# A feature-crossing kernel: SyncE's fill of the first table waits for the second chunk's weights, and the second block's x is loaded behind the last second-half gather

## The chip, the cores and the metric

The kernel runs on one core of a Trainium2 chip. The metric is the device time of one execution in microseconds; the profile adds the span of one profiled execution, counted from the program's first instruction to its last. A core has five engines that run side by side and wait for each other through semaphores: TensorE (PE in the profile; PEld is its weight load), VectorE (DVE), ScalarE (ACT), GpSimd (POOL) and SyncE (SP). Transfers between the device's memory and the on-chip memory are issued by SP, ACT or POOL and carried by the core's 16 DMA engines.

## What is computed

Three layers of a compressed interaction network over x of 1024 samples, 39 fields and 64 embedding columns, then a linear layer over the sums:

```
def _cin_layer(Xk, X0, W, b):
    O = W.shape[0]
    Hk, Fdim = (Xk.shape[1], X0.shape[1])
    Wr = W.reshape(O, Hk, Fdim)
    return jnp.einsum('bhe,bfe,ohf->boe', Xk, X0, Wr) + b[None, :, None]
...
Xk = X0
outs = []
for W, b in ((W0, b0), (W1, b1), (W2, b2)):
    Xk = _cin_layer(Xk, X0, W, b)
    outs.append(Xk.sum(axis=-1))
cin_output = jnp.concatenate(outs, axis=-1)
return cin_output @ fc_w.T + fc_b
```

Everything is float32, and the result has one number for each sample.

## The kernel before

The first layer needs every product of two fields. The kernel folds the weights of all three layers into weights for those pairs at the start, and then works on blocks of 32 samples (2048 columns, a column being one embedding position of one sample). For each block it gathers rows of x into tables of 128 partitions, so that the product of two tables holds 128 pairs of fields at once. Five tables r[0] to r[4] per block, and two small ones u and v per two blocks, cover all pairs. There are 32 blocks, handled in twos: 16 pairs.

**Chunks.** A chunk is one product of two tables (`product`, line 213, on DVE), followed by four matmuls of 128x512 with that chunk's weights (`multiply`, line 555, on TensorE). A block has six chunks; chunk c multiplies tables (0,1), (0,2), (3,1), (3,2), (0,4) and (3,4) in this order, so tables 0 to 3 serve the first four chunks and table 4 is first used by the fifth. The first block of each pair has a seventh step, the product of u and v, for both blocks together (`join`, line 567). The products run four steps ahead of the matmuls (`AHEAD`, line 652) and use four buffers. When a block is done, `finish` (line 613) takes the sums out of the accumulators with ScalarE and VectorE; in the program's order, it stands before the product of the next block's fifth chunk.

**Where the rows come from.** Row gathers read from a table `xd` in device memory, with x laid out by field (40 rows a block: 39 fields and a row of ones; 80 rows for two blocks). There are three such tables, used in turn. A direct load (`load`, line 166) writes one block of x into a table as 1248 runs of 64 numbers. For the very first block there is a shorter way: `load_half` brings its two halves (16 samples, 1024 columns each) into the small tables `xh[0]` and `xh[1]`, and tiles 0 to 3 are gathered from these, half by half (loop at line 389, eight gathers). The first big table is then filled in three ways: the row of ones by `fill_ones(0, ...)`, the first block by copies of the two halves (line 396), and the second block by `load(1)`. Out of it come tile 4 of the first block (`roll(0, (4,))`), u and v (`roll_small(0)`) and the five tiles of the second block (`roll(1)`).

**Order.** The program is scheduled by hand: every engine executes its instructions in the order in which the function records them. POOL issues the indirect gathers (line 174) and some direct DMAs, SP and ACT the others. An instruction that waits holds up what stands behind it on the same engine. Before the change, POOL's order at the start is: `fill_ones(0)`; the four gathers of the first half; two of the second half; `load(1)`; the other two of the second half; tile 4; u; v; the five tiles of the second block; four small loads of biases (b0s, b1s, b2s, fcb); the ones of table 2. SP's order is: the row fc_w; the copies of half 1 and half 0 into table 0, which wait for the halves only; the ones of table 1, which wait for a copy of the ones that ACT makes (line 709); and the loads of blocks 2, 3 and so on.

**TensorE's order at the start.** The weights' preparation; a transpose of chunk 0's weights (`weight_turn`, line 536, whose result two ACT copies at lines 544 and 545 carry over); the first quarter of chunk 0; the transpose of chunk 1's weights; the second quarter of chunk 0 and the first of chunk 1; the transpose for chunk 2; and so on to the main loop at line 689.

```
    for k, (n, c) in enumerate(steps[:3]):
        multiply(n, c, p[n, c], (0,))
        if k < 2:
            weight_turn(steps[k + 1][1])
        multiply(n, c, p[n, c], (1,))
```

Of the kernel before, what the change touches and what calls it, by code (L numbers as in the profile page):

```python
# [54 lines left out]
F32 = mybir.dt.float32  # L55
# [5 lines left out]
B, F, E, H = 1024, 39, 64, 64  # L61
# [25 lines left out]
NY = 3  # L87
# [60 lines left out]
def cin_kernel(ctx: ExitStack, tc: tile.TileContext, x, w0t, b0, w1, b1, w2, b2, fc_w, fc_b, out):  # L148
    nc = tc.nc
# [3 lines left out]
    const = ctx.enter_context(tc.tile_pool(name="const", bufs=1))  # L153
# [6 lines left out]
    xd = [dram.tile([2 * FT, BLK], F32, name=f"xd{k}") for k in range(NTAB)]  # L160
    xh = [dram.tile([F, SUB], F32, name=f"xh{k}") for k in range(2)]

    def bank(name):
        return psum.tile([128, MM], F32, name=name, tag="po")

    def load(n, engine=nc.sync):
        first = n % 2 * FT
        engine.dma_start(  # L168
            xd[n // 2 % NTAB][first : first + F].rearrange("f (b e) -> f b e", e=E),
            xv[:, n * BB : (n + 1) * BB, :],  # L170
        )

    def gather_rows(dst, table, k):
        nc.gpsimd.indirect_dma_start(  # L174
            dst, None, table, bass.IndirectOffsetOnAxis(ap=lists[:, k : k + 1], axis=0)
        )

    def roll(n, tiles=range(NT)):
        for i in tiles:
            k = n % 2 * NT + i  # L180
            gather_rows(rt[n % 2][:, i], xd[n // 2 % NTAB][: FT if k < NT else 2 * FT], k)

    def roll_small(n):
        table = xd[n // 2 % NTAB].rearrange("f (t c) -> (f t) c", c=SUB)
        for k, dst in enumerate((ut, vt)):
            gather_rows(dst[n // 2 % 2], table, 2 * NT + k)
# [6 lines left out]
    b2s = const.tile([H, 1], F32, name="b2s")  # L193
    b1s = const.tile([128, 1], F32, name="b1s")
    b0s = const.tile([128, 1], F32, name="b0s")
    fc0s = columns[:, 1:2]
    fcb = const.tile([NY * 32, 1], F32, name="fcb")
# [7 lines left out]

    ones = const.tile([16, 2, 128], F32, name="ones")
    ones1 = const.tile([16, 2, 128], F32, name="ones1")

    both = const.tile([128, F * FT], F32, name="both")
    pairs = const.tile([128, NCHUNK, 128], F32, name="pairs")  # L210
# [2 lines left out]
    def product(n, c, cols=slice(0, BLK), p=None):  # L213
        if p is None:
            p = prods.tile([128, BLK], F32, name="p", tag="p")
        if c < NPAIR:
            i, k = PAIRS[c]
            r = rt[n % 2]
            nc.vector.tensor_tensor(p[:, cols], r[:, i, cols], r[:, k, cols], ALU.mult)  # L219
        else:  # L220
            nc.vector.tensor_tensor(p[:, 0:SUB], ut[n // 2 % 2], vt[n // 2 % 2], ALU.mult)  # L221
        return p

    prep = tc.tile_pool(name="prep", bufs=1)
    with prep as prep:
# [142 lines left out]
        def fill_ones(k, engine, src):  # L368
            engine.dma_start(xd[k][F::FT].rearrange("r (p c) -> p r c", c=128), src)

        fill_ones(0, nc.gpsimd, ones)


        nc.vector.tensor_scalar(unit, apart, 0, None, ALU.is_equal)
        for h in (0, H):
# [13 lines left out]
        halves = [slice(0, SUB), slice(SUB, BLK)]  # L389
        for k, cols in enumerate(halves):  # L390
            for i in range(4):
                gather_rows(rt[0][:, i, cols], xh[k], i)
                if k and i == 1:
                    load(1, nc.gpsimd)
        for k in (1, 0):
            nc.sync.dma_start(xd[0][0:F, halves[k]], xh[k])
        roll(0, (4,))

# [70 lines left out]
        nc.vector.tensor_tensor(both_of[:, 0:1], most, jumps[:, 0:1], ALU.add)  # L471
        nc.vector.tensor_tensor(both_of[:, 1:2], both_of[:, 0:1], jumps[:, 1:2], ALU.add)
        nc.vector.tensor_scalar(lists[:, 2 * NT :], both_of, 2.0, seat, ALU.mult, ALU.add)
        roll_small(0)
        roll(1)
        for h in (0, H):
            nc.gpsimd.dma_start(b0s[h : h + H], b0.rearrange("(h o) -> h o", o=1))
        nc.gpsimd.dma_start(b1s, b1.rearrange("(h o) -> h o", o=1).to_broadcast([H, 2]))
        nc.gpsimd.dma_start(b2s, b2.rearrange("(h o) -> h o", o=1))
        nc.gpsimd.dma_start(  # L480
            fcb, fc_b.rearrange("(p o) -> p o", o=1).to_broadcast([NY * 32, 1])
        )
        fill_ones(2, nc.gpsimd, ones)
        w1v = w1s.rearrange("o (h f) -> o h f", f=F)
        groups = [(k, min(NA * k, F - NA)) for k in range(4)]
        for k, a in groups:
# [49 lines left out]
    def weight_turn(c):  # L536
        place = len(turned) % 4 * 128
        if not place:
            tr = bank("tr")
        else:  # L540
            tr = turned[-1]
        turned.append(tr)
        nc.tensor.transpose(tr[:, place : place + 128], pairs[:, c], unit)  # L543
        nc.scalar.copy(wa[:, c, 0 : 2 * H], tr[:, place : place + 2 * H])  # L544
        nc.scalar.copy(wa[:, c, 2 * H :], tr[:, place : place + H])
# [5 lines left out]
    def open_block(n):  # L551
        if n not in po:
            po[n] = [bank("po") for _ in range(BLK // MM)]

    def multiply(n, c, p, quarters=range(BLK // MM)):
        open_block(n)
        for m in quarters:
            side = m % 2 * H
            nc.tensor.matmul(  # L559
                po[n][m],  # L560
                wa[:, c, side : side + 2 * H],
                p[:, bass.ts(m, MM)],
                start=n % 2 == 0 and c == 0,
                stop=n % 2 == 1 and c == NPAIR - 1,
            )
# [94 lines left out]
    p = {}  # L660
# [19 lines left out]
    weight_rows(c)  # L680
    p[n, c] = product(n, c, halves[0])
    product(n, c, halves[1], p[n, c])
    for k, (n, c) in enumerate(steps[:3]):
        multiply(n, c, p[n, c], (0,))
        if k < 2:
            weight_turn(steps[k + 1][1])
        multiply(n, c, p[n, c], (1,))

    for at, (n, c) in enumerate(steps[:-TAIL]):
# [116 lines left out]
```

## Time and profile before

| | us |
|---|---|
| median of 3 runs | 733.25 |
| the runs | 733.25, 735.53, 732.84 |
| the profiled execution | 733.14 |
| its span | 731.4 |
| TensorE busy in the span | 724.7 |
| VectorE busy | 638.3 |
| GpSimd busy | 397.6 |
| ScalarE busy | 166.9 |

The profiled execution's own time is 1.7 us above its span, which leaves out what lies before the first and after the last instruction. The granted TensorE clock was 0.997 of full speed over the span.

A row of the timeline has the start, the time from the start of the first instruction merged into it to the end of the last, the engine, the line, the operation, its tiles, how many instructions were merged, and in brackets the idle time of the engine ahead of it with what ended it. A DMA row is its issue, not its transfer. Transfers are seen in the DMA view: the queue q0 is GpSimd's, q1 is SyncE's and q10 is ScalarE's, and for GpSimd's issues the view also has the time from the issue to the landing.

### The profile page before, as it was taken

The page shows a single profiled execution, that of the slowest core. Times are in us where ns is not written, and L with a number is a line of the kernel's source. Part 1 is how long each engine was busy: PE and PEld are TensorE (multiplying, and loading weights), DVE is VectorE, ACT ScalarE, POOL GpSimd, SP SyncE. Part 2 cuts the span into 40 slices and gives each one's busy share as a digit, 9 for nine tenths or more (in the row PEclk, how much of TensorE's full clock was granted, in tenths as well). Part 3 has the DMA queues.
Part 4 walks back from the last instruction along what each step waited for, and adds up shares of the span by engine and source line. Part 5 has one row for each costly group of instructions (what it writes and reads, how often), then busy time and mean ns, then how long its engine had stood idle before and what let it go on. Part 6 is the DMA issues. An engine that isn't in the chain of part 4 may idle for free.

```text
span 731.4 us, 6351 instructions
## 1 busy us (share of the span) xinstructions
PE 724.7 (99%) x2375; PEld 316.1 (43%) x2375; DVE 638.3 (87%) x521; ACT 166.9 (23%) x240; POOL 397.6 (54%) x254
## 2 busy tenths in 40 slices
PE   8999999999999999999999999999999999999998
PEld 4444444444444444444444444444444444444443
DVE  6999798988889988889988889888898988889885
ACT  3332121222212222221222212222121221212222
POOL 6789886536555445754537555455654547545300
PEclk9999999999999999999999999999999999999999
DMA  8997899789575887757679675896767777565700
GB/s 268 376 337 280 315 342 356 290 307 338 232 273 231 281 336 286 270 225 285 269 288 330 223 289 219 304 348 236 268 256 274 301 287 266 224 252 236 288 0 0
DMA packets 65983, 197.24 MB, mean 270 GB/s; under 512 B 40110, under 2 KB 40179, under 8 KB 45984
## 3 DMA queue, kind: packets, MB, share of 16 engines
q0 software_dynamic: 28784, 185.56, 65.5%
q1 hardware_dynamic: 35468, 9.29, 5.5%
q10 hardware_dynamic: 1700, 1.99, 1.0%
q8 instruction: 18, 0.29, 0.1%
q14 instruction: 13, 0.11, 0.0%
HBM read 196.76 MB, written 10.60 MB: 284 GB/s over the span
## 4 chain that ended last, share of the span: by engine, by line
PE 99%; DVE 0%; DMA 0%; issue 0%; ACT 0%; DVEq 0%
PE po L559 91%; PE po L579 4%; PE po L590 2%; PE idle L279 0%; PE pv L406 0%; PE pt L487 0%; PE small L323 0%; PE pv L487 0%; PE pw L418 0%; DMA fcrow<-in_fc_w 0%; PE tr L543 0%; DVE g L609 0%; DVE pairs L526 0%; DVE sums L631 0%; ACT z L607 0%
## 5 line engine op out<-in xcount | busy, mean ns | idle before, releaser
L559 PE MATMUL po<-p,wa 128*128 128x512 f32 x1536 | 666.0, 594 | 0.0
L219 DVE TENSOR_TENSOR p<-r 128x2048 f32<-128x2048 f32 (+2 forms) x198 | 434.1, 2224 | 72.4 <-PE po L559 67.1
L559 PEld LDWEIGHTS po<-p,wa 128*128 128x128 f32 x1536 | 290.5, 190 | 371.7 <-issue 354.6
L174 POOL DMA_INDIRECT r<-xd,lists x156 | 302.3, 1938 | 267.1 <-issue 266.2
L607 ACT ACTIVATE z<-po,columns 64x512 f32<-64x512 f32 x128 | 87.3, 682 | 380.1 <-PE po L590 217.9
L609 DVE SCALAR_TENSOR_TENSOR g<-po,b0s,z 64x512 f32<-64x512 f32 x128 | 95.9, 749 | 9.3 <-ACT z L607 5.3
L602 ACT COPY g<-r 39x1024 f32<-39x1024 f32 x64 | 66.7, 1043 | 155.0 <-DVE sums L620 126.8
L620 DVE TENSOR_REDUCE sums<-g 103x16 f32<-103x1024 f32 x62 | 75.6, 1220 | 2.1
L174 POOL DMA_INDIRECT u<-xd,lists x16 | 38.9, 2432 | 7.5 <-issue 4.6
L174 POOL DMA_INDIRECT v<-xd,lists x16 | 38.5, 2403 | 4.9 <-issue 4.9
L579 PE MATMUL po<-p,wa 32*64 32x512 f32 x512 | 31.6, 600 | 0.0
L221 DVE TENSOR_TENSOR p<-u,v 128x1024 f32<-128x1024 f32 x16 | 19.5, 1218 | 0.0
L579 PEld LDWEIGHTS po<-p,wa 32*64 32x64 f32 x512 | 9.4, 131 | 20.2 <-issue 19.4
L590 PE MATMUL po<-u,wa 32*64 32x512 f32 x256 | 17.0, 587 | 0.0
L174 POOL DMA_INDIRECT r<-xh,lists x8 | 8.0, 996 | 4.8 <-DVE tmp L387 2.7
L590 PEld LDWEIGHTS po<-u,wa 32*64 32x64 f32 x256 | 5.7, 132 | 8.0 <-issue 8.0
L526 DVE TENSOR_TENSOR pairs<-both 128x2 f32<-128x2 f32 (+27 forms) x59 | 6.1, 171 | 0.2
L544 ACT COPY wa<-tr 128x128 f32<-128x128 f32 x8 | 2.1, 266 | 16.2 <-PE tr L543 16.2
L279 PE MATMUL idle<-const-float32-1.0 128*128 128x256 f32 (+1 forms) x8 | 4.0, 596 | 0.8 <-PEq L793 0.8
L543 PE MATMUL tr<-unit,pairs 128*128 128x128 f32 x8 | 2.4, 294 | 2.2 <-DVE pairs L526 2.2
L543 PEld LDWEIGHTS tr<-unit,pairs 128*128 128x128 f32 x8 | 1.2, 151 | 4.7 <-ACT pairs L524 2.7
L168 POOL DMA_DIRECT2D xd<-in_x x3 | 3.2, 1055 | 0.0
(97 smaller groups left out, 56.7 us busy)
## 6 DMA issues: line engine op xcount, KB each, us to landing
xd<-in_x SPq DMA_DIRECT2D x28, 312.0 KB
r<-xd,lists POOLq DMA_INDIRECT x156, 8.9
xd<-in_x POOLq DMA_DIRECT2D x3, 312.0 KB, 7.6
w2s<-in_w ACTq DMA_DIRECT2D x1, 624.0 KB
w1s<-in_w ACTq DMA_DIRECT2D x1, 624.0 KB
w0s<-in_w0t ACTq DMA_DIRECT2D x1, 380.2 KB
xh<-in_x ACTq DMA_DIRECT2D x2, 156.0 KB
xd<-xh SPq DMA_DIRECT2D x2, 156.0 KB
```

The source lines that it names most:

```text
L174: nc.gpsimd.indirect_dma_start(dst, None, table, bass.IndirectOffsetOnAxis(ap=lists[:, k : k + 1], axis=0))
L219: nc.vector.tensor_tensor(p[:, cols], r[:, i, cols], r[:, k, cols], ALU.mult)
L221: nc.vector.tensor_tensor(p[:, 0:SUB], ut[n // 2 % 2], vt[n // 2 % 2], ALU.mult)
L279: nc.tensor.matmul(idle[:, 0:cols], nc.const_aps.tensor(1.0, (128, 128), F32), nc.const_aps.tensor(1.0, (128, cols), F32), start=True, sto ...
L526: nc.vector.tensor_tensor(out, diagonal(a, b, sa, sb), diagonal(b, a, sb, sa), ALU.add)
L559: nc.tensor.matmul(po[n][m], wa[:, c, side : side + 2 * H], p[:, bass.ts(m, MM)], start=n % 2 == 0 and c == 0, stop=n % 2 == 1 and c == NP ...
L579: nc.tensor.matmul(dst[half * H : half * H + H], wa[rows, NPAIR, at : at + H], p[rows, bass.ts(side, MM)], start=t >= 2, stop=t < 2 and ha ...
L590: nc.tensor.matmul(dst[half : half + H], wa[rows, NPAIR + 1, H : 2 * H], ut[n // 2 % 2][rows, bass.ts(side, MM)], start=False, stop=t < 2,)
L602: nc.scalar.copy(gt[H : H + F], rt[n % 2][0:F, 0, bass.ts(m, SUB)])
L607: nc.scalar.activation(z[one], po[n][m][other], AF.Identity, bias=fc0s[other])
L609: return lambda: nc.vector.scalar_tensor_tensor(g[n][m // 2][0:H, at], po[n][m][one], b0s[one], z[one], ALU.add, ALU.mult)
L620: nc.vector.tensor_reduce(sums[:, b_at : b_at + SB], g[n][m // 2].rearrange("p (b e) -> p b e", e=E), AX.X, ALU.add,)
```

## The change

SyncE's fill of the first table is put into a function, `fill_table`, which is called right after the transpose of the second chunk's weights. In it a copy of the ones is made on ScalarE (`ones0`), and SyncE's DMA of that copy is now the first of its three DMAs into table 0; so they wait for ScalarE to reach that point of its order, behind the copies of the second chunk's weights. Before, the ones went out on GpSimd, from `ones` itself, and SyncE's copies waited for the halves alone. The instructions of GpSimd that follow (tile 4, u and v, the second block's tiles, the biases, the ones of table 2) stand in the same order as before and are recorded in `fill_table`, too. `load(1)` moves from between the second and third gathers of the second half to behind the fourth.

```diff
@@ const tiles
     ones1 = const.tile([16, 2, 128], F32, name="ones1")
+    ones0 = const.tile([16, 2, 128], F32, name="ones0")
@@ preparation
-        fill_ones(0, nc.gpsimd, ones)
...
         for k, cols in enumerate(halves):
             for i in range(4):
                 gather_rows(rt[0][:, i, cols], xh[k], i)
-                if k and i == 1:
-                    load(1, nc.gpsimd)
-        for k in (1, 0):
-            nc.sync.dma_start(xd[0][0:F, halves[k]], xh[k])
-        roll(0, (4,))
+        load(1, nc.gpsimd)
...
-        roll_small(0)
-        roll(1)
-        for h in (0, H):
-            nc.gpsimd.dma_start(b0s[h : h + H], b0.rearrange("(h o) -> h o", o=1))
...
-        fill_ones(2, nc.gpsimd, ones)
@@ after the products of the first four chunks
+    def fill_table():
+        nc.scalar.copy(ones0, ones)
+        fill_ones(0, nc.sync, ones0)
+        for k in (1, 0):
+            nc.sync.dma_start(xd[0][0:F, halves[k]], xh[k])
+        roll(0, (4,))
+        roll_small(0)
+        roll(1)
+        for h in (0, H):
+            nc.gpsimd.dma_start(b0s[h : h + H], b0.rearrange("(h o) -> h o", o=1))
...
+        fill_ones(2, nc.gpsimd, ones)
+
     for k, (n, c) in enumerate(steps[:3]):
         multiply(n, c, p[n, c], (0,))
         if k < 2:
             weight_turn(steps[k + 1][1])
+        if k == 0:
+            fill_table()
         multiply(n, c, p[n, c], (1,))
```

More of the change, by code (lines that the diff above doesn't have):

```diff
@@ L473, in cin_kernel @@
         nc.vector.tensor_scalar(lists[:, 2 * NT :], both_of, 2.0, seat, ALU.mult, ALU.add)
-        roll_small(0)
-        roll(1)
-        for h in (0, H):
-            nc.gpsimd.dma_start(b0s[h : h + H], b0.rearrange("(h o) -> h o", o=1))
[L478 to L482, printed above, removed]
-        fill_ones(2, nc.gpsimd, ones)
         w1v = w1s.rearrange("o (h f) -> o h f", f=F)
@@ L682, in cin_kernel @@
     product(n, c, halves[1], p[n, c])
+    def fill_table():
[8 more added lines that the diff above has]
+            nc.gpsimd.dma_start(b0s[h : h + H], b0.rearrange("(h o) -> h o", o=1))
+        nc.gpsimd.dma_start(b1s, b1.rearrange("(h o) -> h o", o=1).to_broadcast([H, 2]))
+        nc.gpsimd.dma_start(b2s, b2.rearrange("(h o) -> h o", o=1))
+        nc.gpsimd.dma_start(
+            fcb, fc_b.rearrange("(p o) -> p o", o=1).to_broadcast([NY * 32, 1])
+        )
+        fill_ones(2, nc.gpsimd, ones)
     for k, (n, c) in enumerate(steps[:3]):
```

## The prediction

> **What bounds the kernel now.** I read the page's busy line first, then the chain of waits in order of time, then the first 60 us engine by engine on the timeline, and last the DMA view in short windows. All durations below are of the one profiled execution (733.14 us, span 731.4); the median of the runs is 733.25, so a change worked out on the span can be added to the median as it stands.
>
> ```profile
> PE 724.7 (99%) x2375; PEld 316.1 (43%) x2375; DVE 638.3 (87%) x521; ACT 166.9 (23%) x240; POOL 397.6 (54%) x254
> ```
>
> TensorE is busy all the time. A busy TensorE can hide waits inside modelled matmuls, so the chain has to confirm it (start, length, what; all us):
>
> ```profile
> 15.39 0.37 DVE pairs L526 x3
> ...
> 16.30 0.14 issue
> 16.43 0.30 PE tr L543
> 16.73 0.61 PE idle L279 x2
> 17.34 1.82 PE po L559 x2
> 19.16 0.21 PE tr L543
> 19.38 2.23 PE po L559 x4
> ...
> 21.71 6.87 PE po L559 x16
> ...
> 43.06 41.40 PE po L559 x96
> ```
>
> From 16.43 to 726.24 every piece is TensorE's, with no wait between. 41.40 us for 48 matmuls of 128x512 (two passes each, 96) is 0.8625 us a matmul; the sixteen passes at 21.71 keep the same pace (6.87/16 = 0.43). Only the first six run slower, 1.82 for two passes and 2.23 for four: 1.5 us more than at the later pace. The windows view gives a granted clock of 0.50 from 18 to 20 us, so that is the clock and not a wait for data. Before 16.43 the chain holds the weights' preparation on PE, DVE and ACT, and of DMAs the small row fcrow only. So the x traffic that the change moves is not on the path now. It can come onto it, and to see how far away it is one needs POOL's and DVE's order:
>
> ```profile
> 17.10 1.25 POOL L174 DMA_INDIRECT r<-xh,lists  x1 [0.31 <-issue]
> 18.65 1.66 POOL L174 DMA_INDIRECT r<-xd,lists  x1 [0.30 <-issue]
> 23.23 0.94 POOL L174 DMA_INDIRECT u<-xd,lists  x1 [2.92 <-DVE p L219]
> 24.47 0.95 POOL L174 DMA_INDIRECT v<-xd,lists  x1 [0.30 <-issue]
> 25.73 0.96 POOL L174 DMA_INDIRECT r<-xd,lists  x1 [0.30 <-issue]
> ```
>
> ```profile
> 23.38 2.50 DVE L219 TENSOR_TENSOR p<-r 128x1024 f32<-128x1024 f32 x2 [0.72 <-DMA r<-xh,lists]
> ...
> 29.77 2.28 DVE L219 TENSOR_TENSOR p<-r 128x2048 f32<-128x2048 f32 x1
> ...
> 37.22 2.29 DVE L219 TENSOR_TENSOR p<-r 128x2048 f32<-128x2048 f32 x1 [0.39 <-DMA r<-xd,lists]
> 39.80 2.29 DVE L219 TENSOR_TENSOR p<-r 128x2048 f32<-128x2048 f32 x1 [0.29 <-DMA r<-xd,lists]
> 42.42 4.50 DVE L219 TENSOR_TENSOR p<-r 128x2048 f32<-128x2048 f32 x2 [0.33 <-DMA r<-xd,lists]
> ...
> 52.35 11.09 DVE L219 TENSOR_TENSOR p<-r 128x2048 f32<-128x2048 f32 x5
> ```
>
> POOL idles 2.92 us before u. The label says DVE, but the instruction also waits for the landing of block 1's load, issued at 14.45 with 7.6 us to landing, and the program text has that dependence. DVE waits 0.72 us for a second-half gather, then three times for the gathers of the other set of tables (block 1's): those are DMA-paced, one every 2.6 us.
>
> [...]while SyncE's two copies moved (14 to 17.2 us) their queue took 25.7% of the engines and POOL's fell to 75.6%, from 93.6% in 10.2 to 14.[...]
>
> **The change, part by part.**
>
> 1. fill_ones(0) leaves POOL (0.76 us at 3.70). POOL then waits 2.71 us, until 7.17, for lists and half 0. Gain nothing.
>
> 2. load(1) goes behind the last second-half gather: it costs POOL 1.06 us plus 0.3, so the third and fourth gathers (15.81, 17.10) are issued some 1.06 us earlier. SyncE's 312 KB also leave the DMA engines in 14 to 17.2 us: 25.7% of 3.2 us is 0.8 us of all engines. Load(1)'s own place in the queue was 1.1 us (landings: 13.51 + 7.5 = 21.0, 14.45 + 7.6 = 22.1). So the third gather lands about 1.9 us earlier than 23.3 and DVE's 0.72 us wait is gone. TensorE needs that product (chunk 1, third quarter) at 21.71 + 5 x 0.8625 = 26.0, and half of the 2.50 us pair is done by 24.6: slack 1.4. Gain on the path nothing; what is late next is DVE's product of chunk 4.
>
> 3. The copy into ones0 on ACT: 0.40 us, by the same copy at line 709. ACT is free from 19.79 and idle until 21.75, 1.96 us. Cost nothing; without this cover it would delay the third chunk's weights by 0.4.
>
> ```profile
> 19.57 0.22 ACT L545 COPY wa<-tr 128x64 f32<-128x64 f32 x1
> 21.75 0.27 ACT L544 COPY wa<-tr 128x128 f32<-128x128 f32 x1 [1.96 <-PE tr L543]
> ```
>
> 4. SyncE now waits for that copy, to 20.2. It issues the ones (0.35) and the two copies (1.70, as at 10.13), and is done at 22.3. Queued behind are the ones of table 1 and the loads of blocks 2 and 3, which before began at 24.60 when ACT was ready: not delayed. Waiting for it is POOL's gather of r tile 4, and behind that u, v, the five gathers of the other set, the biases and the ones of table 2.
>
> When do the copies land? Issued at 10.13 they first moved at 14: 3.9 us. From 20.6 that makes 24.5; from an emptier queue earlier. Through load(1) and the copies the transfers are the same set, and before they ended with the last second-half gather at 17.10 + 7.5 = 24.6. I take 25.2 for the landing, bounds 24.2 (no dead time) and 27.5 (the full 5.2 us from the end of the second issue to the last packet, as before: 11.8 to 17).
>
> 5. Tile 4. Gather from 25.3, first data some 1.5 us later (7.17 to about 8.7 for the first gather), then 2.5 us for 1 MB (24.6 to 18.65 + 8.5 = 27.15 before), 0.2 for the end: 29.5. DVE wants it at 29.05 to 29.77, with TensorE's need of that product at 30.52 + 3 x 0.8625 = 33.1 against its end at 32.05: slack 1.05. Holds until the gather starts at about 26.5.
>
> 6. u, v and the other set. All of this is one DMA stream: before, tile 4's data began at 24.6 and the fourth gather landed at 42.3, 17.7 us. Now it begins at 25.3 + 1.5 = 26.8 and the fourth lands at 44.5: 2.2 us later (a start at 24.3 would give 1.2, one at 27.6 gives 4.5). DVE's row moves with it: products (1,2) and (1,3) from 44.6, the finish of block 0 (46.84 to 52.35 now, 5.5 us), then (1,4), which ends at 52.35 + 2.29 = 54.64 now and 56.8 then. TensorE starts (1,4) at 43.06 + 16 x 0.8625 = 56.86. Slack before 2.2, after about nothing. (1,0) to (1,3) have 3.5 to 6.5. Block 2's gathers land 55.1 for a product needed at 63.76: safe. So the path pays from 0 to 0.2, and by the bounds 0 to 2.3. Afterwards DVE, faster than TensorE, catches up: at 63.89 it already waits for TensorE.
>
> Sum on 733.14: 0 + 0 + 0 + 0 + 0 + 0.15 = 733.3; on the median 733.4.
>
> **Rivals.** *Late table* (slower): the copies, stuck behind POOL's traffic, land at 26.5 or later. For it: 7 us from first issue to last packet last time. Against: POOL's queue now runs dry at about 24. Each us beyond 25.2 goes straight to TensorE at (1,4): 26.5 gives 1.3 us, 734.7. To be 0.5% slower (3.7 us), the gather would have to start near 28.9; that decides it, and nothing in the trace shows such a delay.
>
> *Earlier start* (faster): without the copies and load(1) the half gathers land sooner, and the front shortens. For it: DVE's 0.72 us wait, the only wait for data before 30 us. If all of it were on the path, 732.5. With a half-rate window shorter by all its 1.5 us besides, 731.0. Against: TensorE has no gap there, and its first matmul follows weights.
>
> *The change does not do what it says*: POOL waited until 23.23 for load(1) anyway, so delaying the copies to about then moves only tile 4, and the stream keeps its order: 733.25.
>
> **How the numbers follow.** About nothing lost 0.60, late table 0.25, earlier start 0.11, no effect 0.04. Prediction 733.4. The range must take in the late case up to 27.5 (2.3 us, 735.5; one run before stood at 735.53 by itself) and most of the early one: 732.0 to 735.5. About 0.5%, 3.7 us, is what a measurement of this kernel can tell from no change; only extremes of the cases reach it: faster 0.03 (window and wait together, and more), slower 0.05 (a gather start past 28.9), same 0.92.
>
> **What would show it.** Right: TensorE gapless from 16.43; no DVE wait near 23; POOL's first xd gather at 24.3 to 26 and u right behind it; DVE waits for r<-xd near 39 to 45, about 2 us later than now; DVE's finish of block 0 near 49. A late table shows as a TensorE gap before line 559 near 57, or near 33. Wrong: the chain leaving 16.43, a TensorE wait elsewhere, or a gather start past 27.

## The result: slower by 0.6 %, and where the time went

| | before | after |
|---|---|---|
| median, us | 733.29 | 738.23 |
| range of the six runs, us | 732.82 to 735.53 | 736.95 to 738.74 |
| profiled execution, us | 733.14 | 738.55 |
| its span, us | 731.4 | 736.8 |

The ratio is 1.0061, with a 95% interval of 1.0046 to 1.0076. The changed kernel is slower by 4.9 us, more than the 0.5% that can be told from no change and outside the range of the prediction.

The busy line of the changed kernel hardly shows it. TensorE is as busy as before and 5.4 us of span have come on top:

```profile
PE 725.1 (98%) x2375; PEld 314.6 (43%) x2375; DVE 638.1 (87%) x521; ACT 167.1 (23%) x241; POOL 400.3 (54%) x253
```

The chain of waits (start, length, what) shows it at once. Before, it was TensorE's alone from 16.43 on. Now it leaves TensorE again after the first matmuls:

```profile
14.38 0.30 PE tr L528
...
17.68 0.29 ACT ones L670
...
19.41 6.51 DMA xd<-xh
...
26.66 6.75 DMA r<-xd,lists
...
33.53 2.30 DVE p L220
...
35.97 2.05 PE po L544 x2
```

It is best read backwards. The first matmuls of chunk 4, the fifth one, start at 35.97, when their product is done; the product waited for the gather of tile 4; the gather for SyncE's copies; the copies for ScalarE's copy of the ones, the one that the change added. (Line numbers are the changed kernel's: 220 is the product, 544 the matmul, 564 and 575 the join, 670 the new copy.) In the timeline the same stop stands in three places (start, time, engine, and in brackets the idle time ahead). GpSimd:

```profile
26.66 2.21 POOL L174 DMA_INDIRECT r<-xd,lists  x1 [7.31 <-DMA xd<-xh]
...
57.23 14.66 POOL L174 DMA_INDIRECT u<-xd,lists  x1 [0.30 <-issue]
...
72.19 0.93 POOL L174 DMA_INDIRECT v<-xd,lists  x1 [0.30 <-issue]
```

VectorE, at its wait for tile 4 and beside that long u:

```profile
33.53 2.29 DVE L220 TENSOR_TENSOR p<-r 128x2048 f32<-128x2048 f32 x1 [4.95 <-DMA r<-xd,lists]
...
57.79 13.29 DVE L220 TENSOR_TENSOR p<-r 128x2048 f32<-128x2048 f32 x6
```

TensorE has these two waits where it had none:

```profile
35.97 2.05 PE L544 MATMUL po<-p,wa 128*128 128x512 f32 x2 [4.42 <-DVE p L220]
...
106.36 27.73 PE L544 MATMUL po<-p,wa 128*128 128x512 f32 x64 [0.59 <-DVE p L220]
```

The second wait has a chain of its own. Behind the first block the chain leaves TensorE again, and before it comes back it runs through the u of 14.66 us:

```profile
47.70 0.67 ACT z L592
...
57.23 8.10 POOL u L174
...
104.03 2.29 DVE p L220
...
106.36 27.73 PE po L544 x64
```

The stop also costs something afterwards. In the windows view (window, its length, busy time of PE, PEld, DVE, ACT, POOL, then the granted clock, the DMA share and GB/s) the array runs at half rate right behind it, where the kernel before had 1.00:

```profile
36.00:38.00 2.00, 2.00 (x3) 0.86 (x4) 2.00 (x10) 0.00 (x0) 1.70 (x2) 0.50 1.03 434
```

While GpSimd waited, its DMA queue q0 had next to nothing to move (2.9% of the engines from 24 to 26), and nothing behind the wait until 29.5. The DMA view from 26 to 28 us (packets, MB, share of the 16 engines), first of the changed kernel, where only SyncE's small-packet loads of blocks 2 and 3 moved:

```profile
q1 hardware_dynamic: 1406, 0.36, 78.4%
```

and then of the kernel before, which at that time moved tile 4 and what followed it:

```profile
q0 software_dynamic: 186, 0.69, 91.8%
```

Added up, with places of TensorE's order in both traces (the join's first matmul stands at 40.30 before and 44.92 after, its third at 128.61 and 134.09):

| | us |
|---|---|
| first transpose at 14.38 instead of 16.43 | -2.05 |
| wait for tile 4's product | +4.42 |
| half rate behind it and what else lies before the first join, by difference: 44.92 - 40.30 + 2.05 - 4.42 | +2.25 |
| wait at 106.36 | +0.59 |
| the rest, not assigned | +0.2 |
| span, 736.8 - 731.4 | +5.4 |

The windows put about 1.5 of the 2.25 us on the clock: 36 to 38 at 0.50 is 1.0 us lost, 38 to 40 at 0.75 another 0.5. The first term is not the change's: an early front came in kernels with and without it (first transpose near 14.4 in the kernel before with one small addition below, at 15.98 in e2 below, which keeps the whole wait).

### The profile page after: what moved, and what is told of

It is laid out like the page before. It is cut to its first block, busy times and chain, and to the rows that moved or that the text cites. A ratio compares the mean times of both kernels' runs of the same rounds, so it can differ in the third digit from the quotient of the medians.

```text
span 736.8 us, 6354 instructions
## 1 busy us (share of the span) xinstructions
PE 725.1 (98%) x2375; PEld 314.6 (43%) x2375; DVE 638.1 (87%) x521; ACT 167.1 (23%) x241; POOL 400.3 (54%) x253
## 4 chain that ended last, share of the span: by engine, by line
PE 88%; DMA 5%; issue 2%; DVE 2%; POOL 2%; ACT 0%; SPq 0%; DVEq 0%; POOLq 0%
PE po L544 81%; PE po L564 4%; DMA r<-xd,lists 3%; PE po L575 2%; POOL u L174 1%; DVE p L220 1%; DMA xd<-xh 1%; DMA xd<-in_x 1%; DVE g L594 1%; POOL r L174 0%; PE pv L401 0%; PE idle L280 0%; PE pt L472 0%; ACT z L592 0%; PE small L324 0%
## 5 line engine op out<-in xcount | busy, mean ns | idle before, releaser
L174 POOL DMA_INDIRECT r<-xd,lists x156 | 315.2, 2020 | 270.6 <-issue 254.4
L174 POOL DMA_INDIRECT v<-xd,lists x16 | 26.5, 1658 | 4.9 <-issue 4.9
L564 PEld LDWEIGHTS po<-p,wa 32*64 32x64 f32 x512 | 9.4, 131 | 20.2 <-issue 20.2
```

The source lines that it names most:

```text
L174: nc.gpsimd.indirect_dma_start(dst, None, table, bass.IndirectOffsetOnAxis(ap=lists[:, k : k + 1], axis=0))
L564: nc.tensor.matmul(dst[half * H : half * H + H], wa[rows, NPAIR, at : at + H], p[rows, bass.ts(side, MM)], start=t >= 2, stop=t < 2 and ha ...
```

## The experiments

Theory A of the expectations: SyncE's wait is the cause, since GpSimd and the DMA engines stand still until the copies land. Theory B: `load(1)`'s new place is the cause. A third came out of the first runs: a gather that GpSimd starts while VectorE multiplies cannot proceed until VectorE pauses. (From l1 and l2 on, most expectations call this one A, and D its rival, a full DMA queue; where A is something else, the expectation says what.) Each ratio is against runs of the kernel before on the same chip. The waits are those of one profiled run each, without the one ahead of the first transpose, which every kernel has; g1's is the fastest of its eight runs (734.49) and e7's the slowest of its ten (736.62), so these two traces aren't typical of their medians.

| kernel | median, us (runs) | ratio, 95% interval | TensorE's waits in the profile, us |
|---|---|---|---|
| e1_load_only | 738.85 (6) | 1.0056 [1.0030, 1.0083] | 2.65 at 45.28, 1.13 at 60.41, 1.72 at 106.56 |
| e2_wait_only | 738.35 (11) | 1.0063 [1.0044, 1.0082] | 3.28 at 36.01 |
| e3_loads_after_tables | 736.27 (20) | 1.0028 [1.0012, 1.0044] | 3.88 at 34.61 |
| e4_wait_first_chunk | 737.98 (8) | 1.0050 [1.0023, 1.0078] | 0.73, 0.32, 1.85, 1.58 |
| e5_load_moved_pause | 736.50 (18) | 1.0039 [1.0027, 1.0051] | 1.04, 0.88, 1.90 |
| b2_load_by_sync | 739.16 (14) | 1.0074 [1.0058, 1.0090] | 2.20, 1.45, 1.47 |
| g1_changed_with_gaps | 737.11 (8) | 1.0040 [1.0025, 1.0056] | 2.99 at 34.29 |
| g2_before_with_gaps | 732.97 (22) | 0.9984 [0.9976, 0.9992] | 0.54 at 29.96 |
| b1_before_spins | 734.72 (13) | 1.0005 [0.9992, 1.0017] | 3.82 at 18.54 |
| g3_before_spins_gaps | 733.25 (14) | 0.9994 [0.9983, 1.0004] | 2.14 at 17.36 |
| e6_load_moved_gaps | 734.55 (13) | 1.0019 [1.0009, 1.0029] | 1.14 at 58.56 |
| e7_loads_after_gaps | 735.07 (10) | 1.0024 [1.0014, 1.0035] | 3.07 at 34.56 |

l1_one_input and l2_two_inputs ran once each and are read from their traces alone.

**Only the load moved.** The kernel before, with the second part of the change and nothing else:

```diff
                 gather_rows(rt[0][:, i, cols], xh[k], i)
-                if k and i == 1:
-                    load(1, nc.gpsimd)
+        load(1, nc.gpsimd)
```

> The kernel before with load(1) alone moved behind the fourth second-half gather; SyncE's copies as before. Theory A (the table is filled late because SyncE waits, tile 4 comes late and TensorE stops for it): this part is harmless, the time stays within 1 us of before (732.3 to 734.3) and TensorE has no wait for tile 4's product. Theory B (load(1) behind the gathers is what delays tile 4, u and v): 736.5 to 738.5, with the wait of POOL's first big-table gather as long as in the changed kernel (7.3 us).

It costs as much as the whole change, so that theory A alone falls. But tile 4 is on time (its gather begins at 18.06), so B as stated falls, too. What is late is u and all behind it. GpSimd's timeline of this kernel:

```profile
25.64 3.26 POOL L174 DMA_INDIRECT u<-xd,lists  x1 [5.65 <-DVE p L219]
29.20 2.60 POOL L174 DMA_INDIRECT v<-xd,lists  x1 [0.30 <-issue]
32.10 2.70 POOL L174 DMA_INDIRECT r<-xd,lists  x1 [0.30 <-issue]
```

and VectorE's, at the same time:

```profile
25.58 2.35 DVE L219 TENSOR_TENSOR p<-r 128x1024 f32<-128x1024 f32 x2
```

In the kernel before, u went out at 23.23 in 0.94 us. Now `load(1)` is issued at 16.69 and not at 14.45 and lands later, u starts at 25.64, 0.06 us after the fourth chunk's product has begun, and takes until after its end. v and r are drawn out in the same way by the next products. Three gathers cost 8.6 us where they cost 2.9. The kernel before has drawn-out gathers, too (3.09, 2.61 and 2.70 us), but further back, at the second to the fourth table of the second block. So here the gathers of its first two tables start 6.4 and 8.1 us later (32.10 and 35.11, against 25.73 and 27.00), and that of the last only 2.5. TensorE meets it 20 us further on:

```profile
45.28 14.00 PE L558 MATMUL po<-p,wa 128*128 128x512 f32 x32 [2.65 <-DVE p L219]
```

**Only the wait.** The changed kernel with `load(1)` back between the second and third gathers of the second half:

```diff
-        load(1, nc.gpsimd)
+                if k and i == 1:
+                    load(1, nc.gpsimd)
```

> The changed kernel with load(1) put back between the second and third gathers of the second half; SyncE still waits for ScalarE. Theory A: most of the loss stays, 736 to 738.5, POOL waits 6 us or more ahead of tile 4's gather and TensorE stops for 3 us or more before line 544. Theory B: the loss goes, 732.5 to 734.

```profile
36.01 1.75 PE L545 MATMUL po<-p,wa 128*128 128x512 f32 x2 [3.28 <-DVE p L220]
```

TensorE's timeline has the changed kernel's stop, in a front that starts near the kernel before's (first transpose at 15.98), and the clock is 0.58 and 0.57 in the two windows behind it. GpSimd waits 6.18 us for the copies and starts tile 4 at 26.03. So either part costs about 5 us by itself, and both together no more. The trace of the changed kernel has u right behind tile 4, with no wait of its own (29.18, 0.94 us), so that the later landing of `load(1)` no longer shows.

**Are SyncE's loads in the way of tile 4?** The loads of blocks 2 and 3, the traffic that moved while q0 was empty, go to GpSimd behind all tables:

```diff
         fill_ones(2, nc.gpsimd, ones)
+        for k in (2, 3):
+            load(k, nc.gpsimd)
...
-            for k in (2, 3):
-                load(k)
```

> The changed kernel with the loads of blocks 2 and 3 issued by GpSimd behind the second block's tiles in place of by SyncE right behind the copies (same loads, same bytes). Theory A with a queue effect (the 2496 packets of 256 B of these loads, which moved at 24 to 29 us, hold up the copies' landing and tile 4's data): tile 4 lands about 2 us sooner than 33.1 us, TensorE's stop falls from 4.4 to 2 us or less, 734 to 736. Theory A without it (only the late issue and the gather's own 6.4 us count): tile 4 lands as late as before, 737 to 738.5.

The product still starts 6.8 us after its gather (25.38 to 32.17) and TensorE waits 3.88 us, so tile 4's way is hardly shorter than the 6.9 of the changed kernel. Yet the ratio, 1.0028, is under half of the changed kernel's loss (1.0061), and the intervals don't meet. In the traces the stop is 0.5 us shorter and the wait near 106 is gone; whether that is the loads' doing isn't shown. In e2 they do seem to stand in tile 4's way: its gather ended at 26.03 + 1.08 = 27.11, and from 26 to 28 q1 took 79.3% of the engines and q0 moved 2 packets.

**The wait one chunk earlier.** `fill_table()` stands ahead of the loop, so that the copy of the ones follows the first chunk's weights:

```diff
+    fill_table()
     for k, (n, c) in enumerate(steps[:3]):
...
-        if k == 0:
-            fill_table()
```

> The changed kernel with the fill of the table recorded ahead of the first matmuls, so that SyncE waits for the first chunk's weights and not for the second's: about 2.3 us earlier. Theory A: tile 4's gather starts about 2 us earlier, TensorE's stop falls by 2 us or more[...]: 733 to 735.5. Theory B: no change, 737 to 738.5.

The stop for tile 4 shrinks to 0.73 us (gather at 24.63, product at 30.98), and no half rate follows: the eight passes of 128x512 behind it take 3.60 us, as in the kernel before. Yet the time stays. u now starts at 25.93, in a product, and takes 2.91 us; the waits have moved to the second block and to 106. A's expectation missed that; the time is the one that B gave, though B had no change of the stop.

**Is it the two on-chip inputs?** Three operations of the size of half a product, whose result nobody uses, are put on VectorE while GpSimd gathers the first half: a multiplication of two on-chip operands (the same tile twice), or a sum over one.

```diff
...
+        for _ in range(3):
+            nc.vector.tensor_tensor(dummy, flat_pairs, flat_pairs, ALU.mult)
```

> The kernel before with three extra VectorE instructions of about 1.2 us each from about 10 us on, back to back, each multiplying two on-chip operands of 128x1024 into a scratch tile (extra work; the result does not use it). Theory A[...]: the gather that starts at about 11 us takes 2 us or more in place of 0.94, to 0.95 us after the last of the three. Theory D (long gathers come from a full DMA queue and not from VectorE): 0.94 to 1.1 us as before.

```diff
...
+        for _ in range(3):
+            nc.vector.tensor_reduce(dummy, pairs, AX.X, ALU.add)
```

> The same place and about the same VectorE time as in the run with two inputs, but the three extra instructions are sums with one on-chip operand of 128x1024 (extra work; the result does not use it). Theory A: the gathers at 11 to 14 us keep 0.94 us each. Theory D: whatever the two-input run shows, this one shows the same.

The timeline with two inputs:

```profile
9.88 3.74 DVE L477 TENSOR_TENSOR dummy<-pairs 128x1024 f32<-128x1024 f32 x3
10.12 1.80 POOL L174 DMA_INDIRECT r<-xh,lists  x1 [0.30 <-issue]
12.22 0.95 POOL L174 DMA_INDIRECT r<-xh,lists  x1 [0.31 <-issue]
```

and with one:

```profile
10.02 3.72 DVE L476 TENSOR_REDUCE dummy<-pairs 128x8 f32<-128x1024 f32 x3
10.71 0.94 POOL L174 DMA_INDIRECT r<-xh,lists  x1 [0.30 <-issue]
```

One input leaves every gather beside it at 0.94 us. Two hold the first one to the end of the multiplication that was running (9.88 + 3.74/3 = 11.13; the gather ends at 11.92, 0.8 later). The kind was right and the size expected was not: the hold ended with the first of the three. These three depend on each other and take 1.25 us each, the kernel's own products without a pause 4.62/4 = 1.155; through four of those the gather of u in the same trace took 4.25 us. So what frees GpSimd seems to be a small gap between two products. (The two kinds also differ in what they write, 128x1024 against 128x8. Against that as the cause stands the end of block 0 in the changed kernel: VectorE writes 64x512 there, with an accumulator, one on-chip tile and a column of biases as inputs, and the gather that starts at 55.99, beside the second of these, takes 0.93.)

**A pause and a gap.** If that is so, more work on VectorE makes the kernel faster. First e1 with one unused sum of 1.07 us ahead of the fourth chunk's product, timed to let u through; then a write of a single number, 0.06 us, ahead of every product, in the changed kernel (g1), the kernel before (g2) and e1 (e6):

```diff
+    pause = const.tile([128, NCHUNK - 1], F32, name="pause")
+    nc.vector.tensor_reduce(
+        pause, rt[0][:, 0, 0 : 128 * (NCHUNK - 1)].rearrange("p (c n) -> p c n", n=128), AX.X, ALU.add
+    )
     p[n, c] = product(n, c, halves[0])
```

> The kernel with load(1) alone moved (which took 5.6 per mille more than before), plus one extra VectorE sum of about 1.1 us with one on-chip operand ahead of the fourth chunk's product (extra work; the result does not use it). Theory A: the gather of u, which started at 25.64 just inside that product and took 3.26 us, now starts ahead of the product and takes 0.94; v then waits for the product's end; the second block's first gathers are issued some 1.7 us earlier and TensorE's waits of 5.5 us in all shrink by 1 to 3 us: 735 to 738. Theory D: extra VectorE work cannot help; the same or up to 1 us slower, 738.5 to 740.

```diff
+    gap = const.tile([1, 1], F32, name="gap")
...
+        nc.vector.memset(gap, 0.0)
```

> The changed kernel with one more VectorE instruction ahead of every product: a write of a single number into a scratch tile, about 0.06 us (extra work; the result does not use it), so that products never stand back to back. Theory A[...]: the gather of u after the start-up, 14.66 us in the changed kernel, takes under 3.5 us; tile 4's gather takes at most 1.9 in place of 2.2; the second TensorE wait (0.59 us near 106) is gone, and the time falls by 0.5 to 2 us: 736 to 737.8. Theory D (long gathers come from the DMA queue): the long gather stays at 10 us or more and the time is the changed kernel's or up to 1 us more.

> The kernel before with the same small instruction ahead of every product. Theory A: its gathers get shorter too (12.45 us of u in the first pairs to under 3.5), and because TensorE had no wait in the profiled execution the time does not rise for the extra VectorE work: 731.5 to 733.7. Theory D: 733.3 to 735.

> The kernel with load(1) alone moved, plus the small VectorE write ahead of every product (extra work; the result does not use it). Theory A (load(1) costs because u's gather slips into a product and every gather behind it is then held up by the next one): u, v and the second block's first gathers take 0.94 to 1.9 us each where they took 3.26, 2.60 and 2.70, the second block's second gather is issued by 31.5 us and not at 35.1, and most of the 5.5 us of TensorE waits goes: 732.5 to 734.5. Theory E (the later landing of load(1) is enough by itself): waits of 3 us or more stay, 736 or more.

e5: u begins beside the sum and is through in 0.94, v runs into the product behind it and takes 3.02:

```profile
25.50 0.94 POOL L174 DMA_INDIRECT u<-xd,lists  x1 [5.52 <-DVE p L219]
26.74 3.02 POOL L174 DMA_INDIRECT v<-xd,lists  x1 [0.30 <-issue]
```

The kernel took 736.50 with the added work, e1 738.85; TensorE's waits fell from 5.5 us to 3.8, but the intervals of the ratios overlap. With the gaps, the u that took 14.66 us in the changed kernel is done in 0.94, although the same products begin 0.55 us after it; v, which starts inside the first of them, is through at 58.27, 0.8 after that product's end:

```profile
54.62 0.94 POOL L174 DMA_INDIRECT u<-xd,lists  x1 [0.30 <-issue]
55.87 2.40 POOL L174 DMA_INDIRECT v<-xd,lists  x1 [0.30 <-issue]
```

and the wait near 106 is gone. In e6, TensorE's waits fall from 5.5 us in e1 to 1.14, and the ratio from 1.0056 to 1.0019, with intervals that just do not meet (1.0030 and 1.0029). The rest probably belongs to the later landing (u still starts only at 25.89). In the changed kernel the ratio falls from 1.0061 to 1.0040, with intervals that overlap; the stop for tile 4 remains there (2.99 us, in the fastest run). The kernel before gains, too, 0.9984, and is the best of all, so that 0.16% in each of these ratios may be the gaps' own and not the cure of the change. Where that gain lies isn't shown: TensorE had no wait in the profile of before that the gaps could have taken away. The fastest runs of both are alike (732.37 before, 732.34 with gaps); what the gaps lack are the long runs, 734.00 at most against 737.11. What they do to the gathers is plain: in g2 the 16 gathers of u take 0.94 us on average, where before the median was 1.89 and the longest 12.45. Others are still held, but in the stretches seen in g1 and e6 over one product only: the r at 59.64 in g1 and at 60.69 in e6 take 3.11 and 3.10 us, about a product's 2.29 and 0.8 more, where before one r took 7.26. In g2's groups (busy time and mean ns behind the bar, then the idle time) the large gathers take 1714 ns on average:

```profile
L174 POOL DMA_INDIRECT r<-xd,lists x156 | 267.4, 1714 | 331.9 <-issue 318.7 <-DVE gap L217 12.6 <-DVE g L611 0.6
```

against 1938 in the kernel before.

**The hold-up and the loads taken out together.** e3 with the gaps:

> The changed kernel with the loads of blocks 2 and 3 behind the second block's tiles and with the small VectorE write ahead of every product (extra work; the result does not use it). Theory A for tile 4 (the DMA engines run dry while GpSimd waits for the copies[...]): tile 4's gather takes 0.95 to 1.5 us, its product starts 5 to 6 us after the gather and not 6.7, TensorE's stop is 2.5 us or less, 734 to 735.5. If the dead time alone counts[...]: stop of 3.5 to 4.4 us, 736 to 738.

The median, 735.07, lies where theory A had it; the ratio of 1.0024 cannot be told from e3's 1.0028, so the gaps add nothing clear to the loads' move. The stop was to shrink to 2.5 us at most; in the trace, that of the slowest run, it is 3.07, and the eight passes behind it take 5.00 us against 3.60 in the kernel before. The gather starts at 25.86 and the product at 32.12, 6.3 us later, 4.6 after the gather's end, on DMA engines that were empty until its own data came. Their view from 24 to 28 us:

```profile
q0 software_dynamic: 3, 0.01, 0.6%
```

So most of tile 4's way is the time that one gather alone needs through an idle queue. In e7, q0 moves no packet from 26 to 28 and 63 from 28 to 30, so the first of them comes at least 2.1 us after the gather's start. Why that takes so long isn't shown.

**Two misses.** `load(1)` issued by SyncE, to take it out of GpSimd's way:

```diff
-                if k and i == 1:
-                    load(1, nc.gpsimd)
         for k in (1, 0):
             nc.sync.dma_start(xd[0][0:F, halves[k]], xh[k])
+        load(1)
         roll(0, (4,))
```

> The kernel before with load(1) issued by SyncE behind its two copies, not by GpSimd. Theory A: u and v no longer wait for a late load(1) and GpSimd saves a 1.06 us issue, so u is issued at about 20 to 21 us, the tables of the second block come 2 us or more earlier, no TensorE wait appears, and the time is that of before or up to 1.5 us less[...]: 731.5 to 733.5. Theory B (moving load(1) at all costs): 736 or more.

It is the slowest of all. SyncE issued the load at 10.93, and u could start only at 28.01, 7.62 us after GpSimd had nothing else to do. Issued by GpSimd in the kernel before, the same load landed in 7.6 us. Here q1 moved it in a trickle until about 24 (162 packets from 18 to 20, 294 from 20 to 22, 537 from 22 to 24, 48 in the next two us); why u came some 4 us later still is open. And five more of the program's unused matmuls (`spin`) stand ahead of the first weights' transpose, alone and with the gaps, to fill the idle 2.18 us there. Behind these the kernel before has a granted clock of 0.72, 0.50 and 0.93 in the three windows of 2 us from 16 on, together 1.7 us lost:

```diff
         if not k:
+            spin(5, MM // 4)
             weight_turn(c)
```

> The kernel before with five dummy matmuls of 128x128 into the idle bank in TensorE's gap of 2.18 us ahead of the first weight transpose (extra work; the result does not use it). If the idle gap is what puts TensorE at half rate for the 3.4 us from 16.9 us on, the window goes and the time falls by up to 1.7 us, 731.5 to 733; if the demand then meets late tables, part of it is given back.

> Both of the above on the kernel before: dummy matmuls in TensorE's gap and the small VectorE instruction ahead of every product. Theory A: the earlier start is not given back to late tables: 731 to 732.5, the fastest of all. Theory D: as the run with dummy matmuls alone or slower.

They did not remove the half rate at the start: in b1 the first two passes of 128x512 take 2.08 us, in g3 the third takes 1.03, where two take 1.02 in the kernel before (39.27). In b1 ScalarE took over the first weights only at 18.23, after 5.03 us of idling that the trace puts down to nothing in the program, and TensorE waited 3.82 us for it; in g3 ScalarE idled 3.34 us in the same place and TensorE 2.14. Why is open.

## Why the prediction was wrong

Steps 1 and 3 agree with the trace: nothing shows of the ones leaving GpSimd, and ScalarE's copy, 0.29 us, fits into its pause of 1.86. It matters only as what SyncE waits for.

Step 4 was right in the landing, in the profiled run by luck: the copies land at 25.9, inside 24.2 to 27.5, but SyncE issued its first DMA at 17.99 and not at 20.2, and from there the copies took 7.9 us, not the 5.0 of the step. Where the front starts as late as before, it holds to 0.7 us without luck: in e2 SyncE issues at 19.93 and tile 4's gather starts at 26.03, where the step has 25.3. Its premise is wrong: "the same set" of transfers left no room for a GpSimd queue that stands still, and from 24 to 26 us q0 used 2.9% of the engines.

**The step that failed is 5.** It gave tile 4 4.2 us from the gather's start (25.3) to the landing (29.5), composed of the first-data time of the very first gather, a half one (1.5), the transfer time of a tile in a running stream (2.5) and 0.2 for the end. It took 6.9.

The DMA view of the changed kernel tells the three terms apart. No packet of q0 moves from 26 to 29.5, which is 2.8 us after the gather's start; 1.01 of the tile's 1.05 MB move from 29.5 to 32.5, some 3.0 us; the product starts at 33.53, 1.0 us after that. Of the first term some 1.3 us is hold-up that the step did not have: the gather takes 2.21 us and not 0.94, to 1.0 behind the end of VectorE's products at 27.87. In e2, where it takes 1.08, the loads of blocks 2 and 3 fill the engines behind it instead (q1 79.3% from 26 to 28).

In the six kernels of these runs in which SyncE's copies wait, the product starts 6.3 to 7.5 us after the gather, also in the front of e2 (7.5). "Holds until the gather starts at about 26.5" falls with it. The gather came at 26.66, and the price was 4.4 us and a half-rate window, which no step had. With 4.2 us the product could have started at 30.9 and the matmuls 2.4 later, as here, at 33.3, while TensorE ran out of work at 35.97 - 4.42 = 31.55. So in this early front 1.8 us would have been lost even then. In a front like the one before (2.05 later), nothing.

Step 6 took the stream as one of constant length. With the gather late, the finish of block 0 begins at 52.27 instead of near 49. No wait follows near 57, because TensorE has been put back by as much. The slack that it names for the second block was real, though: e1 uses it up, with waits at 45.28 and 60.41.

Step 2's "Gain on the path nothing" holds inside the full change, where u stands behind tile 4. As a statement on `load(1)`'s move it is wrong, as e1 shows: it looked at who comes earlier by the move and not at what u, released later, would run beside. The trace before had the sign of it. There a u beside five products took 12.45 us:

```profile
51.80 12.45 POOL L174 DMA_INDIRECT u<-xd,lists  x1 [0.30 <-issue]
```

Of the rivals, *late table* had the sign and the place ("a TensorE gap near 33"), and its price was too small. 26.66 should have cost 1.5 us by "each us beyond 25.2", and the deciding point of 28.9 was never reached. *Earlier start* did happen, by 2 us, but without the change as well.

**The hold-up and the half rate.** l1 and l2 show the hold-up for one gather: 0.94 us beside a VectorE operation with one on-chip input, 1.80 beside one with two. It lasts over all products that follow each other without a gap: the six from 57.79 end at 71.08, and u ends at 57.23 + 14.66 = 71.89. Behind the later stops, half-rate stretches followed waits of 3.07 us (e7, eight passes in 5.00 us and not 3.60), 3.28 (e2, a clock of 0.58 and 0.57), 3.88 (e3, eight passes in 4.56) and 4.42 (the changed kernel, 0.50 and 0.75), and none of 2.99 or less (g1, 1.00 from 34 to 38; e1, 1.00 from 45 to 49 behind 2.65). The length alone doesn't decide it: at the start of every trace the array runs at half rate, too (two passes in 1.89 to 2.08 us, in g3 one in 1.03), in most of them behind 2.2 to 2.5 us of idling and in g3 behind 1.07 and 2.14. What sets it isn't shown.

## What to carry to other kernels

Here the price of a GpSimd gather depended on what VectorE did when it started: 0.94 us by itself, 14.66 beside six products without a gap. Before moving one, or moving what releases it, look in the timeline at what it will run beside, and look for gathers of many times the shortest length. When a wait leaves a DMA queue empty, the first transfer afterwards is to be priced from an empty queue (6.3 us from the gather's start to the product in e7), not by its share of a running stream (4.2 in the prediction), and a TensorE stop like the ones of 3.07 to 4.42 us here may bring a half-rate window with it. Where products run back to back on VectorE, a tiny write between them is worth a trial: it made even the kernel before faster, 0.9984 [0.9976, 0.9992], in runs that lack the long ones of the kernel before, though the traces do not show where that time lay.

## What was not expected of the hardware

- An indirect gather that takes 0.94 us by itself took 14.66 beside six products of two on-chip inputs without a gap, though its record starts 0.56 us before theirs. A VectorE write of one number in 0.06 us between them was enough to bring u back to 0.94; a gather that starts inside a product is still held until that product ends (2.40).
- One gather of a full tile needed 4.6 us from its end on GpSimd to the product's start even with the DMA engines idle until its data came (e7).
- The load of one block in 256-byte runs, issued by SyncE at 10.93 beside GpSimd's gathers, moved in a trickle until about 24 (162 packets from 18 to 20, 537 from 22 to 24), and u, which needs it, started at 28.01; issued by GpSimd it had landed in 7.6 us.
